# Turning layer 1's weights on VectorE and through DRAM instead of on TensorE, in the opening of a two-layer graph attention kernel

## The chip, the cores and the metric

The kernel runs on one core of a Trainium2 chip. A core has five engines that run their own instruction queues in order: TensorE (PE, matrix products into PSUM), VectorE (DVE), ScalarE (ACT), GpSimd (POOL) and SyncE (SP, which here issues every transfer). What counts is the device time of one execution in microseconds. Before the change it is 2786.34 us, the median of 3 runs (2786.06 to 2786.69).

## The reference

The input x is 128 graphs of 128 nodes with 512 features, in float32; adj is a 128x128 mask for each graph. Two attention layers follow each other.

```python
def _layernorm(x, eps=1e-5):
    return (x - mean(x)) / sqrt(var(x) + eps)

# layer 0: 4 heads of 64, INNER = 256
q, k, v = split_heads(x @ Wq), split_heads(x @ Wk), split_heads(x @ Wv)
attn = softmax(where(adj, q @ k.T / 8, -finfo.max))
x = _layernorm(x + (attn @ v) @ Wo + bo)

# layer 1: 8 heads of 64, INNER = 512, with a layer norm of its own in front
h = (x - mu) * rsqrt(var + 1e-5) * gamma + beta
q, k, v = split(h @ w_qkv.T, 3)
probs = softmax(where(adj | eye, q @ k.T / 8, -1e9))
x = _layernorm(x + (probs @ v) @ w_out.T + b_out)
```

Layer 0's weights come with the features along the rows, as TensorE wants them. Layer 1's w_qkv (1536x512) and w_out (512x512) are used transposed, so the kernel has to turn them once.

## The kernel before

The 128 graphs are 64 groups of G = 2. The order of all instructions is written out by hand (a manual schedule): every engine runs its own in the order in which the Python code emits them. `opening()` prepares weights and begins groups 0 and 1, `step(s)` runs for s from 2 to 63, and `closing` and `last` drain the pipeline. In step s, layer 0's q, k, v of group s are computed (`product_0`), with the softmax of group s - 1, the attention and output product of group s - 2 and its normalisation; layer 1's q and k of group s - 2 (`qk`), the softmax and v of group s - 3, and the attention and output product of group s - 4.

**Products with seven multiplications.** All projections use Strassen's scheme with Winograd's sums: a product of two-by-two blocks in seven block products instead of eight. `INTO` says into which PSUM bank each of the seven goes: 1, 6, 7 and 4 accumulate in bank a, 2 in bank c, 5 and 3 in bank f. The intermediate values are copied out between the accumulations: after product 1, ScalarE copies bank a to e1 (L387 in layer 0, L348 in layer 1, where the copies are called eqk or ev), and only then may product 6 accumulate into that bank. The scheme needs sums of input blocks, made by GpSimd for each group (`halves_sums`, L285: xs of the inputs, so of the attention's output), and sums of weight blocks, made once: four subtractions on VectorE (`combine`, L168 to L171) for layer 0's q, k, v weights, for each layer's output weights, and for layer 1's q, k and v weights. The first block is changed in place.

**Turning of weights.** `load_transposed` (L114) loads w_qkv and w_out in 16 row blocks of 128x512 into tiles that are free at the start (buffers of the groups' rows, tag r, and three others). Its `part(r)` turns one block: four TensorE transposes against the identity (L126) into one of four PSUM buffers, then one copy by ScalarE or VectorE (L130 to L134). `prepare(n)` takes n of these parts from a list. It stands six times in `opening` (12 blocks: q, k and v), and in step 2 takes the rest: gamma and beta (L143) and the four blocks of w_out.

**Turning of data, for groups after the first.** `turn` (L207) turns a group's rows in another way: VectorE transposes 32x32 blocks (L212) into a "turned" tile, of which there are two; SP writes it to DRAM (`put`, L197) and reads it back in four transfers that put the blocks in place (`fetch`, L203) into a "raw" tile, of which there is one; ScalarE brings it into order (L239 for layer 0, L251 for layer 1). Groups 0 to 2 of layer 0 and 0, 1 of layer 1 are turned by TensorE (`transposed`, L228; `finish_direct`, L263).

**Step 2 around layer 1's first product.** GpSimd's order is: so of group 0, the softmax's multiplication (L507), the roots for group 0's normalisation (L608 to L623), ratios, two memsets, xs of layer 1. ScalarE's norms (L634) wait for the roots, `finish_direct`'s transposes for the norms; ScalarE and VectorE then write xT, and `qk` begins with products 1, 2 and 6.

**Transfers.** The program gives transfers eight semaphores in turn, so the issue of each waits for the landing of the eighth before it.

## Time and profile before

| | |
|---|---|
| median of 3 runs | 2786.34 us |
| the profiled execution, its time | 2786.63 us |
| its span, first to last instruction | 2784.5 us |
| granted TensorE clock | 1.000 |
| busy PE / DVE / ACT / POOL | 2768.7 / 1795.3 / 1502.0 / 1747.4 us |
| DMA, mean over the span | 146 GB/s |
| opening, up to the first scores of step 2 | 0 to 38.46 us |
| step 2, up to step 3's last scores | 38.46 to 73.5 us |
| step 3 | 73.5 to 109.25 us |
| step 4, and each step after | 42.84 us |

The page has busy time by engine, the span in 40 slices, transfers, the chain of work that ended last (followed back from the last instruction), and groups of equal instructions. A timeline row has start, duration, engine, line, operation, output<-input, and in brackets the idle time before it with what ended it. A row of busy time by stage has the stretch, its length, then busy us of PE, PEld, DVE, ACT and POOL with the number of instructions, the granted clock, the busy share of the DMA engines and GB/s. In the first 110 us TensorE waits on others for about 4.7 us for the first rows and for 3.4 us more, in pieces of at most 1.0.

### The profile page before, as it was taken

To read this page: it belongs to the slowest core of one execution; us is meant where nothing else is said; L and a number is where in the kernel's file an instruction comes from. 1 tells how busy PE (TensorE), PEld (TensorE's weight loads), DVE (VectorE), ACT (ScalarE), POOL (GpSimd) and SP (SyncE) were. 2 spreads that over 40 slices of the span, in tenths; PEclk is the share of its full clock that TensorE was granted. 3 is DMA by queue.
4 is the path that set the end of the run, shared out by engine and by line. 5 is a ranking of instruction groups with operands and counts; after the bars stand their busy time and mean duration, and the time that the engine had idled before them with its cause. 6 is when DMAs were issued, how large, how long until landed. Compare 5 with 4: busy or idle time off the path is not lost.

```text
span 2784.5 us, 63222 instructions
## 1 busy us (share of the span) xinstructions
PE 2768.7 (99%) x23317; PEld 2609.6 (94%) x23317; DVE 1795.3 (64%) x3307; ACT 1502.0 (54%) x4811; POOL 1747.4 (63%) x2307
## 2 busy tenths in 40 slices
PE   8999999999999999999999999999999999999998
PEld 8999999999999999999999999999999999999997
DVE  5766666666666666666666666666666666666665
ACT  3555555645555556455555564555555645555554
POOL 4566566666665666666656666666566666666664
PEclk9999999999999999999999999999999999999999
DMA  5355454464454544645545445455454464554532
GB/s 169 109 144 165 129 165 148 127 176 140 143 165 128 166 148 127 179 137 143 164 127 168 147 129 175 139 145 165 127 167 146 129 177 135 147 163 128 160 107 69
DMA packets 281796, 405.24 MB, mean 146 GB/s; under 512 B 44680, under 2 KB 206480, under 8 KB 281488
## 3 DMA queue, kind: packets, MB, share of 16 engines
q1 hardware_dynamic: 281488, 401.20, 49.2%
q8 instruction: 185, 3.03, 0.5%
q14 instruction: 123, 1.01, 0.1%
HBM read 205.00 MB, written 196.08 MB: 144 GB/s over the span
## 4 chain that ended last, share of the span: by engine, by line
PE 96%; DVE 1%; issue 0%; POOL 0%; DMA 0%; ACT 0%; SPq 0%; POOLq 0%; ACTq 0%; DVEq 0%
PE qka L322 16%; PE a L378 12%; PE oa L416 12%; PE qkf L322 8%; PE va L322 8%; PE av L568 6%; PE f L378 6%; PE of L416 6%; PE qkc L322 4%; PE vf L322 4%; PE c L378 3%; PE oc L416 3%; PE sc L449 2%; PE sc L455 2%; PE vc L322 2%; PE sc_a L455 2%
## 5 line engine op out<-in xcount | busy, mean ns | idle before, releaser
L507 POOL TENSOR_TENSOR sm<-sm,rec 128x1024 f32<-128x1024 f32 x192 | 364.1, 1896 | 383.1 <-DVE rec L506 382.7
L498 ACT ACTIVATE sm<-sm,nmax 128x128 f32<-128x128 f32 x1536 | 595.4, 394 | 4.6 <-DVE nmax L489 3.7
L589 POOL TENSOR_TENSOR r<-r,bias 128x1024 f32<-128x1024 f32 x128 | 302.2, 2361 | 63.5 <-ACT r L588 63.5
L420 DVE TENSOR_TENSOR r<-oa,r 128x256 f32<-128x256 f32 x508 | 212.1, 418 | 200.3 <-PE oa L416 192.7
L285 POOL TENSOR_TENSOR xs<-xT 128x256 f32<-128x256 f32 x256 | 188.7, 737 | 218.3 <-ACT xT L239 165.1
L498 ACT ACTIVATION_READ_ACCUMULATOR sm<-sm,nmax 128x1 f32 x1536 | 295.9, 193 | 0.0
L348 ACT COPY eqk<-qka 128x512 f32<-128x512 f32 x128 | 74.9, 585 | 349.2 <-PE qka L322 349.2
L483 DVE COPY_PREDICATED sm<-m,sc 128x512 f32<-128x512 uint8 x256 | 172.8, 728 | 135.4 <-PE sc L449 134.9
L322 PE MATMUL qka<-xs,wsqk 128*128 128x128 f32 x2048 | 249.7, 275 | 0.1
L322 PE MATMUL qkf<-xs,w 128*128 128x128 f32 x2048 | 249.8, 275 | 0.0
L522 DVE STREAM_TRANSPOSE turnedp<-sm 128x1024 f32<-128x1024 f32 x189 | 233.9, 1238 | 15.2 <-DMA scrp<-turnedp 10.9
L322 PEld LDWEIGHTS qka<-xs,wsqk 128*128 128x128 f32 x2048 | 239.0, 192 | 0.3 <-POOL xs L285 0.3
L322 PEld LDWEIGHTS qkf<-xs,w 128*128 128x128 f32 x2048 | 239.0, 192 | 0.0
L353 DVE TENSOR_TENSOR qk<-qka,eqk 128x512 f32<-128x512 f32 x64 | 44.3, 691 | 290.4 <-PE qka L322 290.4
L489 DVE TENSOR_REDUCE nmax<-sm 128x8 f32<-128x1024 f32 x192 | 226.2, 1205 | 0.1
L416 PE MATMUL oa<-wso,so 128*128 128x256 f32 x760 | 206.0, 380 | 0.7 <-DVE r L420 0.7
L416 PE MATMUL of<-wo,so 128*128 128x256 f32 x760 | 205.5, 379 | 0.0
L608 POOL TENSOR_SCALAR ve<-mv 128x2 f32<-128x2 f32 x191 | 41.0, 214 | 261.5 <-DVE mv L601 255.4
L634 ACT ACTIVATE r<-r,shift,root 128x512 f32<-128x512 f32 x254 | 192.4, 807 | 8.7 <-POOL shift L623 4.7
L469 POOL MEMSET sm<- 128x1024 f32 x192 | 178.8, 951 | 0.0
L600 DVE BATCH_NORM_STATS2 st<-r 128x6 f32<-128x512 f32 x254 | 171.6, 676 | 4.4
L416 PEld LDWEIGHTS of<-wo,so 128*128 128x128 f32 x760 | 144.2, 190 | 19.9
(155 smaller groups left out, 6801.4 us busy)
## 6 DMA issues: line engine op xcount, KB each, us to landing
scrp<-turnedp SPq DMA_DIRECT2D x189, 512.0 KB, 3.2
pT<-scrp SPq DMA_DIRECT2D x756, 128.0 KB, 4.0
scr<-turned SPq DMA_DIRECT2D x121, 512.0 KB, 4.4
raw<-scr SPq DMA_DIRECT2D x484, 128.0 KB, 3.6
r<-in_x_dram SPq DMA_DIRECT2D x64, 512.0 KB, 3.9
out_dram<-r SPq DMA_DIRECT2D x63, 512.0 KB, 4.9
m<-in_adj_dram SPq DMA_DIRECT2D x64, 32.0 KB, 3.6
raw_r<-in_L_gnn_w_qkv_dram SPq DMA_DIRECT2D x8, 256.0 KB, 4.1
```

The costliest lines, as they stand in the source:

```text
L285: nc.gpsimd.tensor_tensor(o, a0, a1, op=op)
L322: nc.tensor.matmul(o, lhsT, rhs, start=first and n == 0, stop=n == len(todo) - 1, skip_group_check=True)
L378: nc.tensor.matmul(acc[:, t * P:(t + 1) * P], lhsT, rhs, start=first and n == 0, stop=n == len(todo) - 1, skip_group_check=True)
L416: nc.tensor.matmul(acc, left[:, c], right[:, c], start=first and c == 0, stop=c == hk - 1, skip_group_check=True)
L420: nc.vector.tensor_add(part, acc, part)
L469: nc.gpsimd.memset(sm, NEG1 if part else NEG0)
L489: nc.vector.tensor_reduce(NMAX[part], SM[part], AX.X, ALU.max, negate=True)
L498: nc.scalar.activation(sm[:, i, k, :], sm[:, i, k, :], AF.Exp, bias=nmax[:, i, k:k + 1], accum_out=total[:, i, k:k + 1])
L507: nc.gpsimd.tensor_tensor(SM[part], SM[part], rec[:, :, :, None].to_broadcast([P, 2, K1, N]), op=ALU.mult)
L522: nc.vector.transpose(t.rearrange("p q (h r) -> p q h r", r=32), SM.pop(part).rearrange("p i k (q r) -> p q (i k) r", r=32))
L589: nc.gpsimd.tensor_tensor(R[g], R[g], (bias0, bias1)[l][:, None, :].to_broadcast([P, G, E]), op=ALU.add)
L634: nc.scalar.activation(R[g][:, b], R[g][:, b], AF.Identity, bias=shift[:, b:b + 1], scale=root[:, b:b + 1])
```

## The change

The 64 transposes of layer 1's weights on TensorE are gone. The weights are loaded in eight pairs of row blocks (six of w_qkv, two of w_out). For each pair, `turn_rows` transposes it on VectorE and writes it to DRAM, `rows_arrive` reads it back into the one raw tile, and `rows_in_order` copies it into place on ScalarE. These three are placed by hand: pairs 0 and 1 (q) in `opening`, 2 and 3 (k) up to the middle of step 2, 4 and 5 (v) at the end of step 2, 6 and 7 (w_out) at the end of step 3. Group 0's q, k and v are computed by plain products (`plain_0`), which need no sums. The sums of layer 0's q and k weights and of layer 1's q and k weights are made on GpSimd, in whole tiles; v's and the output weights' stay on VectorE. Group 0's rows are loaded graph by graph, its mask after the weights, and the loads of wo, biases, gamma and beta stand later on SP.

```diff
@@ -61,16 +61,15 @@
 
     R, M = {}, {}
 
...
+    WROWS = [six.tile([P, 2, E], F32, tag="r", name=f"raw_{i}") for i in range(4)]
+    rows_ = one.tile([P, 4, E], F32, tag="qk1", name="raw_4")
+    WROWS += [rows_[:, :2], rows_[:, 2:]]
+    WROWS += [one.tile([P, 2, E], F32, tag=t, name=f"raw_{t}") for t in ("v1", "xT1")]
+
+    def load_rows(*pairs):
+        for i in pairs:
+            w, at = (w_qkv, i) if i < 6 else (w_out, i - 6)
+            nc.sync.dma_start(WROWS[i], w[at * 2 * P:(at + 1) * 2 * P].rearrange("(b p) e -> p b e", p=P))
 
     def load(g):
         if g >= NG:
@@ -80,7 +79,10 @@
         nc.sync.dma_start(R[g], x[g * G:(g + 1) * G].rearrange("b n e -> n b e"))
         nc.sync.dma_start(M[g], adj[g * G:(g + 1) * G].rearrange("b i j -> i b j"))
 
-    load(0)
+    R[0] = six.tile([P, G, E], F32, tag="r", name="r_0")
+    M[0] = six.tile([P, G, N], U8, tag="m", name="m_0")
+    for b in range(G):
+        nc.sync.dma_start(R[0][:, b], x[b])
 
 
     ident = const.tile([P, P], F32, name="ident")
@@ -97,46 +99,27 @@
     for h in range(2):
         for i, w in enumerate((wq, wk, wv)):
             nc.sync.dma_start(w0[:, :, h, i, :], w[:, h * HF:(h + 1) * HF].rearrange("(c p) f -> p c f", p=P))
+    nc.sync.dma_start(M[0], adj[:G].rearrange("b i j -> i b j"))
+    load_rows(0, 1, 2, 3)
     load(1)
     wo0 = const.tile([P, INNER[0] // P, E], F32, name="wo0")
-    nc.sync.dma_start(wo0, wo.rearrange("(c p) f -> p c f", p=P))
     bias0 = const.tile([P, E], F32, name="bias0")
-    nc.sync.dma_start(bias0, bo[None, :].to_broadcast([P, E]))
     bias1 = const.tile([P, E], F32, name="bias1")
-    nc.sync.dma_start(bias1, b_out[None, :].to_broadcast([P, E]))
 
     w1 = const.tile([P, KC, 3 * INNER[1]], F32, name="w1")
     wo1 = const.tile([P, INNER[1] // P, E], F32, name="wo1")
     gb_raw = const.tile([2 * KC, P], F32, name="gb_raw")
     gb = const.tile([P, 2 * KC], F32, name="gb")
 
-    setup = []
-    def load_transposed(dst, src, name, scaled=0):
...
-
-    nc.sync.dma_start(gb_raw[:KC], gamma.rearrange("(c p) -> c p", p=P))
-    nc.sync.dma_start(gb_raw[KC:], beta.rearrange("(c p) -> c p", p=P))
+    def wo0_and_bias():
+        nc.sync.dma_start(wo0, wo.rearrange("(c p) f -> p c f", p=P))
+        nc.sync.dma_start(bias0, bo[None, :].to_broadcast([P, E]))
+
+    def other_weights():
+        load_rows(4, 5, 6, 7)
+        nc.sync.dma_start(gb_raw[:KC], gamma.rearrange("(c p) -> c p", p=P))
+        nc.sync.dma_start(gb_raw[KC:], beta.rearrange("(c p) -> c p", p=P))
+        nc.sync.dma_start(bias1, b_out[None, :].to_broadcast([P, E]))
 
     def turn_gamma_beta():
         pt = mm_tile("gb_t")
@@ -154,46 +137,44 @@
     wsqk = const.tile([P, 3, KH, 2, I1 // 2], F32, name="wsqk")
     wsv = const.tile([P, 3, KH, I1 // 2], F32, name="wsv")
 
-    def weight_sums(w, ws, *blocks_):
...
-
-    def weight_sums_0():
-        combine(*(w0[:, c:c + KH, h].rearrange("p c t f -> p c (t f)") for c in (0, KH) for h in range(2)),
-                *(ws0[:, i].rearrange("p c t f -> p c (t f)") for i in range(3)))
+    def combine(eng, *sets):
+
+        for n in range(4):
+            for b11, b12, b21, b22, t2, t3, t4 in sets:
+                o, a, b = ((b12, b12, b11), (t2, b22, b12), (t3, t2, b11), (t4, b21, t2))[n]
+                eng.tensor_tensor(o, a, b, op=ALU.subtract)
+
+    def quarters(w, ws):
+
+        return (*(w[:, c:c + KH, h] for c in (0, KH) for h in range(2)), *(ws[:, i] for i in range(3)))
+
+    def weight_sums_qk(eng, t):
+        combine(eng, quarters(w1qk[:, :, t], wsqk[:, :, :, t]))
+
+    def weight_sums_v():
+        combine(nc.vector, quarters(w1v, wsv))
+
+    def weight_sums_0(eng, lo, hi):
+        combine(eng, tuple(t.rearrange("p c t f -> p c (t f)") for t in (
+            *(w0[:, c:c + KH, h, lo:hi] for c in (0, KH) for h in range(2)),
+            *(ws0[:, i, :, lo:hi] for i in range(3)))))
 
     WSO = tuple(const.tile([P, 3, i // P // 2, E // 2], F32, name=f"wso{l}") for l, i in enumerate(INNER))
 
     def weight_sums_out(l):
         hk = INNER[l] // P // 2
         w = (wo0, wo1)[l]
-        combine(*(w[:, c:c + hk, h * E // 2:(h + 1) * E // 2] for c in (0, hk) for h in range(2)),
-                *(WSO[l][:, i] for i in range(3)))
-
-    load_transposed(w1, w_qkv, "w_qkv", scaled=INNER[1])
-    setup.append(turn_gamma_beta)
-    load_transposed(wo1, w_out, "w_out")
+        combine(nc.vector, (*(w[:, c:c + hk, h * E // 2:(h + 1) * E // 2] for c in (0, hk) for h in range(2)),
+                            *(WSO[l][:, i] for i in range(3))))
 
     WO = (wo0, wo1)
     RATIO, XT, QK, V, QKV = {}, {}, {}, {}, {}
 
 
 
-    def put(t, name):
-
-        scr = dram.tile(list(t.shape), F32, tag=name.split("_")[0], name=name)
+    def put(t, name, bufs=2):
+
+        scr = dram.tile(list(t.shape), F32, tag=name.split("_")[0], bufs=bufs, name=name)
         nc.sync.dma_start(scr, t)
         return scr
 
@@ -218,6 +199,25 @@
             return
         RAW[l] = one.tile([P, 4, G, KC, 32], F32, tag="raw", name=f"raw{l}_{g}")
         fetch(RAW[l].rearrange("p a b c i -> p a (b c i)"), SCR[l])
+
+
+    def turn_rows(*pairs):
+        for i in pairs:
+            t = one.tile([P, 4, G * KC * 32], F32, tag="turned", bufs=2, name=f"turnedw_{i}")
+            for b in range(2):
+                nc.vector.transpose(t.rearrange("p a (b c i) -> p a b c i", b=2, c=KC)[:, :, b],
+                                    WROWS[i][:, b].rearrange("p (c a i) -> p a c i", a=4, i=32))
+            SCR["w", i] = put(t, f"scrw_{i}", 8)
+
+    def rows_arrive(i):
+        RAW["w"] = one.tile([P, 4, 2, KC, 32], F32, tag="raw", name=f"raww_{i}")
+        fetch(RAW["w"].rearrange("p a b c i -> p a (b c i)"), SCR.pop(("w", i)))
+
+    def rows_in_order(i):
+        w, at = (w1, i) if i < 6 else (wo1, i - 6)
+        for b in range(2):
+            o = w[:, :, (2 * at + b) * P:(2 * at + b + 1) * P].rearrange("p c (a j) -> p a c j", a=4)
+            nc.scalar.activation(o, RAW["w"][:, :, b], AF.Copy, scale=SCALE if i < 2 else 1.0)
 
     def transposed(g):
 
@@ -228,7 +228,8 @@
                 nc.tensor.transpose(pt[:, c * N:(c + 1) * N], R[g][:, b, c * P:(c + 1) * P], ident)
             (nc.scalar.copy, nc.vector.tensor_copy)[b](xT[:, :, b * N:(b + 1) * N],
                                                        pt.rearrange("p (c n) -> p c n", c=KC))
-        sums(0, g)
+        if g > 0:
+            sums(0, g)
 
     def in_order(g):
 
@@ -390,6 +391,24 @@
             else:
                 b, h, e = {2: (0, 0, 1), 3: (0, 1, 6), 7: (1, 1, 5)}[i]
                 nc.vector.tensor_add(whole(b, h), src, EV[0, e])
+
+    def plain_0(*what):
+
+        xT = XT[0, 0]
+        for kind, i in what:
+            acc = mm_tile(f"plain_{kind}{i}")[:, :2 * P]
+            for c in range(KC):
+                lhsT, rhs = ((xT[:, c, i * N:(i + 1) * N], w0[:, c, :, 2]) if kind == 2 else
+                             (w0[:, c, i, kind], xT[:, c]))
+                nc.tensor.matmul(acc, lhsT, rhs, start=c == 0, stop=c == KC - 1)
+            acc = acc.rearrange("p (x n) -> p x n", x=2)
+            if kind == 0:
+
+                nc.scalar.activation(QKV[0][:, :, i, 0], acc, AF.Copy, scale=SCALE)
+            elif kind == 1:
+                nc.vector.tensor_copy(QKV[0][:, :, i, 1], acc)
+            else:
+                nc.scalar.copy(QKV[0][:, i, :, 2], acc)
 
 
     def out_product(l, g, *which):
@@ -684,47 +703,48 @@
         for i in which:
             product("qk", g, i)
 
-    def prepare(n):
-        for _ in range(min(n, len(setup))):
-            setup.pop(0)()
-
     def opening():
 
+        QKV[0] = two.tile([P, G, 2, 3, P], F32, tag="qkv0", name="qkv0_0")
+        cleared(1, 0)
         transposed(0)
-        cleared(1, 0)
-
+        turn_rows(0, 1)
+        wo0_and_bias()
+        plain_0((0, 0), (1, 0), (0, 1))
+        turn_rows(2)
+        rows_arrive(0)
+        plain_0((1, 1), (2, 0))
+        turn_rows(3)
+        load(2)
+        other_weights()
         for h in range(2):
             nc.scalar.activation(w0[:, :, h, 0, :], w0[:, :, h, 0, :], AF.Copy, scale=SCALE)
-        product_0(0, 1)
-        weight_sums_0()
-        product_0(0, 2, 5, 6, 3)
-        prepare(2)
-        load(2)
-        product_0(0, 7)
-        prepare(2)
-        product_0(0, 4)
-        transposed(1)
+        weight_sums_0(nc.gpsimd, 0, 2)
 
         made = scores(1)
+        plain_0((2, 1))
         masked(made, 1, 0)
         maxima(1, 0)
+        transposed(1)
+        weight_sums_0(nc.vector, 2, 3)
+        rows_in_order(0)
+        rows_arrive(1)
+        exps(1, 0, 0)
         product_0(1, 1, 2)
-        exps(1, 0, 0, 1)
-        prepare(2)
+        exps(1, 0, 1)
         normalised(1, 0)
         product_0(1, 6, 5)
-        prepare(2)
         weight_sums_out(0)
+        rows_in_order(1)
+        rows_arrive(2)
         addend(0, 0)
-        product_0(1, 7)
-        prepare(2)
+        product_0(1, 7, 3)
         blocks_direct(1, 0)
         cleared(2, 0)
-        weight_sums(w1qk, wsqk, 0)
-        product_0(1, 3)
-        prepare(2)
+        weight_sums_qk(nc.gpsimd, 0)
         product_0(1, 4)
         transposed(2)
+        turn_rows(4, 5)
 
     def step(s):
 
@@ -740,6 +760,9 @@
         if s > 3:
             maxima(s, 1)
         out_sums(0, s - 2)
+        if s == 2:
+            rows_in_order(2)
+            rows_arrive(3)
         exps(s, 0, 0)
         product_0(s, 1)
         exps(s, 0, 1)
@@ -747,6 +770,8 @@
         if s == 3:
             maxima(s, 1)
         maxima(s, 2)
+        if s == 2:
+            turn_rows(6, 7)
         product_0(s, 2)
         normalised(s, 0)
         out_product(0, s - 2, 6, 3)
@@ -754,6 +779,10 @@
         stats(0, s - 2, 0)
         product_0(s, 6)
         exps(s, 1, 1)
+        if s == 2:
+            rows_in_order(3)
+            rows_arrive(4)
+            weight_sums_qk(nc.gpsimd, 1)
         out_product(0, s - 2, 7)
         product_0(s, 5)
         out_product(0, s - 2, 4)
@@ -767,7 +796,10 @@
         flush()
         product_0(s, 4)
         if direct:
-            prepare(len(setup))
+            if s == 2:
+                turn_gamma_beta()
+            else:
+                rows_arrive(6)
         else:
             turn(1, s - 2)
         out_sums(1, s - 4)
@@ -790,7 +822,11 @@
         else:
             finish(s - 2, 0)
         if s == 2:
-            weight_sums(w1qk, wsqk, 1)
+            rows_in_order(4)
+            rows_arrive(5)
+        if s == 3:
+            rows_in_order(6)
+            rows_arrive(7)
         out_product(1, s - 4, 6, 5)
         if not direct:
             finish(s - 2, 1)
@@ -799,6 +835,10 @@
         probs_arrive(s, 1)
         stats(1, s - 4, 0)
         stats(1, s - 4, 1)
+        if s == 2:
+            rows_in_order(5)
+        if s == 3:
+            rows_in_order(7)
         arrive(0, s + 1)
         probs_arrive(s, 2)
         cleared(s + 1, 2)
@@ -810,7 +850,7 @@
         addend(1, s - 3)
         qk(s - 2, 7, 3, 4)
         if s == 2:
-            weight_sums(w1v, wsv, 0, 1)
+            weight_sums_v()
         if s == 3:
             weight_sums_out(1)
```

More of the change, by code (lines that the diff above doesn't have):

```diff
@@ L62 @@
     R, M = {}, {}
-    spare = []
-    def spare_rows(pool, tag, n):
-        rows_n = pool.tile([P, n, E], F32, tag=tag, name=f"raw_{tag}_{len(spare)}")
-        spare.extend(rows_n[:, i] for i in range(n))
-    for i in range(4):
-        spare_rows(six, "r", 2)
-    for tag, n in (("qk1", 4), ("v1", 2), ("xT1", 2)):
-        spare_rows(one, tag, n)
+    WROWS = [six.tile([P, 2, E], F32, tag="r", name=f"raw_{i}") for i in range(4)]
[6 more added lines that the diff above has]
+            nc.sync.dma_start(WROWS[i], w[at * 2 * P:(at + 1) * 2 * P].rearrange("(b p) e -> p b e", p=P))
     def load(g):
@@ L111 @@
     gb = const.tile([P, 2 * KC], F32, name="gb")
-    setup = []
-    def load_transposed(dst, src, name, scaled=0):
-        rows, cols = src.shape
-        raws = []
-        for r in range(rows // P):
-            raw = spare.pop(0)
-            nc.sync.dma_start(raw, src[r * P:(r + 1) * P, :])
-            raws.append(raw)
-        def part(r):
-            raw = raws[r]
-            pt = mm_tile(f"{name}t_{r}")
-            for c in range(cols // P):
-                nc.tensor.transpose(pt[:, c * P:(c + 1) * P], raw[:, c * P:(c + 1) * P], ident)
-            to = dst[:, :, r * P:(r + 1) * P]
-            pt = pt.rearrange("p (c f) -> p c f", f=P)
-            if r * P < scaled:
-                nc.scalar.activation(to, pt, AF.Copy, scale=SCALE)
-            elif r % 2:
-                nc.scalar.copy(to, pt)
-            else:
-                nc.vector.tensor_copy(to, pt)
-        setup.extend(lambda r=r: part(r) for r in range(rows // P))
-    nc.sync.dma_start(gb_raw[:KC], gamma.rearrange("(c p) -> c p", p=P))
-    nc.sync.dma_start(gb_raw[KC:], beta.rearrange("(c p) -> c p", p=P))
+    def wo0_and_bias():
[6 more added lines that the diff above has]
+        nc.sync.dma_start(bias1, b_out[None, :].to_broadcast([P, E]))
     def turn_gamma_beta():
@@ L155 @@
     wsv = const.tile([P, 3, KH, I1 // 2], F32, name="wsv")
-    def weight_sums(w, ws, *blocks_):
-        for c in blocks_:
-            if w is w1qk:
-                b11, b12 = w[:, c, :, 0], w[:, c, :, 1]
-                b21, b22 = w[:, KH + c, :, 0], w[:, KH + c, :, 1]
-            else:
-                b11, b12 = w[:, c, 0], w[:, c, 1]
-                b21, b22 = w[:, KH + c, 0], w[:, KH + c, 1]
-            combine(b11, b12, b21, b22, ws[:, 0, c], ws[:, 1, c], ws[:, 2, c])
-    def combine(b11, b12, b21, b22, t2, t3, t4):
-        nc.vector.tensor_sub(b12, b12, b11)
-        nc.vector.tensor_sub(t2, b22, b12)
-        nc.vector.tensor_sub(t3, t2, b11)
-        nc.vector.tensor_sub(t4, b21, t2)
-    def weight_sums_0():
-        combine(*(w0[:, c:c + KH, h].rearrange("p c t f -> p c (t f)") for c in (0, KH) for h in range(2)),
-                *(ws0[:, i].rearrange("p c t f -> p c (t f)") for i in range(3)))
+    def combine(eng, *sets):
[13 more added lines that the diff above has]
+            *(ws0[:, i, :, lo:hi] for i in range(3)))))
     WSO = tuple(const.tile([P, 3, i // P // 2, E // 2], F32, name=f"wso{l}") for l, i in enumerate(INNER))
```

## The prediction

> **What bounds the kernel now.** I read the page first (busy time, then the chain that ended last), then busy time by stage, then the first 110 us instruction by instruction.

> ```profile
> PE 2768.7 (99%) x23317; PEld 2609.6 (94%) x23317; DVE 1795.3 (64%) x3307; ACT 1502.0 (54%) x4811; POOL 1747.4 (63%) x2307
> ...
> PE 96%; DVE 1%; issue 0%; POOL 0%; DMA 0%; ACT 0%; SPq 0%; POOLq 0%; ACTq 0%; DVEq 0%
> ```

> TensorE holds 96% of the chain. So only two things move the end: TensorE work, and stretches in which TensorE waits. The stages (columns: stretch, its length, then busy us of PE, PEld, DVE, ACT, POOL) are the opening, steps 2 and 3, and step 4:

> ```profile
> 4.70:38.46 33.76, 32.47 (x265) 31.14 (x265) 19.28 (x27) 14.29 (x38) 11.90 (x12) 1.00 0.74 247
> 38.46:73.50 35.04, 33.72 (x310) 32.13 (x311) 25.95 (x49) 13.27 (x36) 19.02 (x26) 1.00 0.25 77
> 73.50:109.25 35.75, 34.69 (x276) 32.01 (x272) 24.27 (x44) 18.70 (x68) 22.76 (x28) 1.00 0.45 125
> 109.25:152.09 42.84, 42.84 (x365) 40.47 (x364) 29.17 (x54) 23.49 (x75) 27.30 (x36) 1.00 0.50 143
> ```

> From step 4 on PE has no idle time (42.84 of 42.84 us), and the change doesn't touch those steps. Whatever shift stands at 109.25 us, where step 4 begins, stands at the end. The ledger is therefore only of the first 109 us. The place that decides most is the start of layer 1's q,k products in step 2 (timeline):

> ```profile
> 57.38 1.51 ACT L268 ACTIVATE xT<-ht,gb 128x128 f32<-128x128 f32 x4
> ...
> 57.90 2.18 PE L322 MATMUL qka<-xT,w 128*128 128x128 f32 x16 [0.16 <-ACT xT L268]
> ...
> 59.91 1.95 PE L322 MATMUL qkc<-xT,w 128*128 128x128 f32 x16
> ...
> 60.17 0.59 ACT L348 COPY eqk<-qka 128x512 f32<-128x512 f32 x1 [1.28 <-PE qka L322]
> ...
> 62.00 2.05 PE L322 MATMUL qka<-xs,wsqk 128*128 128x128 f32 x16
> ```

> Product 1 fills bank qka, product 2 another bank, and product 6 accumulates into qka again. It may not start before ScalarE has copied product 1 out (eqk, L348). Here that copy is done by 60.8, so it costs nothing.

> [...]a 128x256 subtraction, 0.42 us elsewhere, takes 2.47 beside a GpSimd addition of 2.54:

> ```profile
> 30.91 2.54 POOL L589 TENSOR_TENSOR r<-r,bias 128x1024 f32<-128x1024 f32 x1
> ...
> 31.27 2.47 DVE L169 TENSOR_TENSOR wso<-wo 128x256 f32<-128x256 f32 x1
> ```

> [...]Here the smallest read-back needs 2.5 us from issue to landing (the line of L203):

> ```profile
> L203 SPq DMA_DIRECT2D raw<-scr x484: 302/429/1666, 63.4 to 2661.4; - x162
> ...
> DMA to landing us min/median/max: 2.5/3.9/5.7
> ```

> [...]the first a product's 8 matmuls at 7.02 take 2.08 us, the same 8 take 1.16 at 22.71.

> **The change, part by part** (us on before's clock).

> *TensorE work.* 64 transposes go: 16 blocks of four at 0.49 (8 records in 1.04 pitch 0.98) = 7.8; 5.9 of it in the opening, 1.9 in step 2. Group 0's seven products (7 x 1.34 = 9.4) become six plain ones of four 128x256 matmuls (L416 has two such records in 0.43, so 24 x 0.43 = 10.3). Net 6.9 us less work; before also loses 1.0 and 0.7 us to VectorE's weight copies (waits at 39.97 and 35.66). That is the most there is to gain: about 8.6.

> *Opening.* The turning is a chain: load, VectorE transpose (2 x 0.67 by L212), write to DRAM, read back in four transfers, ScalarE reorder (two copies, 1.14 by L239). Two "turned" buffers mean that pair 2 is transposed only when pair 0's write has landed. On SP's queue that write stands behind four 0.52 MB loads, r_1 and a mask. In before Wv landed at 10.9 and loads then ran at 371 to 390 GB/s: 3.2 MB more = 8.4, so 19.3. VectorE turns pair 2 until 20.6, and behind it waits the k copy that the first scores need: scores at 21.0 against 21.62. The products of group 0 themselves are hidden in this. ScalarE now does pair 0's reorder ahead of the exps: read-back lands about 26, so reorder until 27.3, half the exps (1.55) and the copy of product 1 until 29.4, where before it was 24.9. Product 6 of group 1 starts at 29.4 against 26.36; 8.5 us of PE work follow, with 1.2 of waits on VectorE's wo subtractions[...]. The step-2 attention starts at about 40.2 against 41.06: **-0.9**. Of the 5.9 + the waits saved, nearly all is spent waiting.

> *GpSimd, first sums.* Pair 1's read-back stands behind 4.7 MB of 0.52 MB transfers plus 0.3 MB after pair 0's write. At 0.38 MB/us, one read-back at its slower rate (221 GB/s in 104:109, +0.9), its last quarter issues at 33.4 and lands at 36.5; reorder until 37.7. GpSimd's four subtractions of 128x512: rows give 0.46 at 128 columns, 0.73 at 256, 2.36 at 1024, so 1.27 each, 5.3 with gaps: until 43.0. Behind them wait xs (3.2) and so: first so at 46.7. TensorE's third out product wanted it at 44.39. TensorE, there at 43.5, waits 3.2 us, and product 6 of group 2 is at 49.35 against 47.02, the shift now +2.3: **+3.2**. The 1.27 is from rows of other widths; it can't be under the 0.73 of half the width nor over the 1.90 of twice it (L507), so four of them are between 3.0 and 7.8, and the wait between 1 and 6. [...]VectorE's turning of pairs 6 and 7 (2.55) stands in front of the residual adds, on which the seventh out product waits: another **+0.5**, shift +2.8.

> *GpSimd, second sums.* After the normalise (ends about 52.8) four more subtractions, until 58.1, ahead of the roots. Their chain (52.23 to 53.79) ends at 59.7, ScalarE's norms follow, and finish_direct's copies end at 63.2 against 58.89, shift +4.3: **+1.5**, with the 1.9 of missing transposes already in it. Behind the roots on GpSimd stand ratios, two memsets (1.84) and xs; xs still comes before product 6 in its new place.

> *Two round trips.* In step 2 ScalarE has, between those copies and eqk: reorder of pair 4 (1.15); only then the one raw buffer is free and the four read-backs of pair 5 issue (1.4 to the last, +2.9 landing, 4.4 with the hand-over); reorder (1.15); then eqk (0.5). That is 7.2 after the copies' end. Product 2 ends 2.97 after it (61.86 - 58.89). So TensorE stands still for 4.2 us, **+4.1** over before's 0.14. Step 3 does the same with pairs 6 and 7: product 6 was at 100.15, copies' end 97.34 + 7.2 = 104.55: **+4.4**.

> The landing can be 2.5 to 4 us instead of 2.9, so each stall is 3.8 to 5.5.

> *The rest.* v sums in four pieces of 0.69 for eight of 0.43: **-0.4**, VectorE being on the chain there. At nothing I put four edits. The split first load: the turning chain hides it. Mask 0 behind the weights: about 12, wanted at 22. wo, its bias and r_2, now held on SP behind writes that wait for VectorE: about 22 and 29, wanted at 30.6 and 38; each us later than that would cost one. In step 3 SP holds the probabilities' read-backs behind pair 7's, which waits for ScalarE: some 2 us later, wanted 10 us on. GpSimd's first sums (group 0's weights, 16.4 to 21.7) are wanted at 29.4. Half-rate clock[...]: from 0 to about 2 for each of three or four; I take **+1.6** in all.

> Sum: -0.9 +3.2 +0.5 +1.5 +4.1 +4.4 -0.4 +1.6 = +14.0. The span 2784.5 becomes 2798.5. The profiled execution took 2786.63, 2.1 around the span; the runs' median is 2786.34, so 1.84: 2800.3.

> **Rivals.** (a) *Feeds on time*: the transfers of pair 1 land some 6 us earlier and GpSimd's queue stays hidden; then only the round trips count: -0.9 -1.9 +4.1 +4.4 -0.4 = +5.3, 2791.6. For: SP's queue is idle from 25 to 55 in before. Against: the DMA share there is 1.04 until 28 without the added 3 MB. (b) *Faster*: every read-back has landed when ScalarE asks for it, so TensorE's own work sets the pace: the 8.6 us above, 2777.7. The mechanism is the landing time alone, its place the two eqk copies. Pairs 5 and 7 would have to land within about 0.1 us of the issue for no stall; the sign turns where the waits that come in (8.5 in the two stalls alone) fall under the 8.6 of work and waits removed, and less than 3 us of them may be left for 0.2%. Against: 2.5 is the minimum of the 1240 read-backs of L203. (c) *Nothing*: gain and stalls cancel, 2786. (d) *Worse*: written and read-back traffic holds the 221 GB/s for the whole opening, pair 1 is 3 us later, and each long stall pays the full half-rate stretch: +22, 2808. That the turning leaves TensorE is certain from the program's order.

> **How the numbers follow.** Forecast 0.62, (a) 0.13, (b) 0.05, (c) 0.05, (d) 0.15. A measurement tells 0.2% (5.6 us) from no change. Half of (a) and all of (c) are within: same 0.11; faster 0.05; slower 0.84. Range 2790 to 2809, reaching over (a) and (d); the forecast's own is 2795 to 2805.

> **What would show it.** Right: TensorE idle before product 6 of step 2 and of step 3, released by ScalarE's eqk copy, 4 to 6 us each; scores(1) near 21; so late in step 2; step 4's start at about 122 us, and 42.84 us per step after it. Wrong: no idle before those products; pair 1's reorder done by 32; or a step 4 that starts before 109.

## The result, and the profile after

The changed kernel takes **2807.36 us** (median of 4 runs, 2805.98 to 2809.73), beside 2786.52 for the kernel before (2786.06 to 2787.40): a ratio of **1.0075, 95% interval 1.0062 to 1.0088**. The forecast was 2800.3, range 2790 to 2809: sign and range held, the size was 7 us short. The profiled execution took 2805.98, its span 2804.1 against 2784.5 before: +19.6.

From the page of the changed kernel: busy time, the granted clock in 40 slices (the row called PEclk), the chain by engine.

```profile
PE 2772.3 (99%) x23217; PEld 2610.4 (93%) x23217; DVE 1794.3 (64%) x3304; ACT 1504.6 (54%) x4817; POOL 1758.3 (63%) x2315
...
PEclk8999999999999999999999999999999999999999
...
PE 95%; DVE 0%; ACT 0%; issue 0%; POOL 0%; POOLq 0%; ACTq 0%; DVEq 0%
```

TensorE has 100 instructions fewer and yet 3.6 us more of busy time. The counts can't say why; the first digit of the clock can. It is an 8: part of the first 70 us ran at less than the full clock. The chain says as little as it did before, since all the damage is in less than 5% of the span.

Busy time by stage shows where (stretch, length, then PE, PEld, DVE, ACT, POOL with their instructions, granted clock, DMA share, GB/s): everything up to step 4's first scores, and step 4.

```profile
0.00:129.53 129.53, 104.68 (x741) 95.82 (x742) 68.15 (x116) 49.77 (x148) 65.49 (x80) 0.91 0.62 193
129.53:172.40 42.87, 42.87 (x365) 40.50 (x364) 29.41 (x54) 23.49 (x75) 27.32 (x36) 1.00 0.47 135
```

Step 4 takes 42.87 us with TensorE never idle, as before (42.84). So the loss lies ahead of it: step 4 starts at 129.53 where it started at 109.18, **+20.35** (behind it single steps of one kernel or the other take 0.3 to 0.4 us more, so that +19.6 of it stand in the span). In those 129.53 us TensorE is idle for 24.85. What it waits for there (waiting for: us in all, times, longest):

```profile
PE qka L323 <- ACT eqk L349: 7.6, 2, 4.5
PE sc L468 <- DVE qkv L409: 3.7, 1, 3.7
PE of L435 <- POOL so L286: 3.7, 1, 3.7
PE xt L228 <- DMA r<-in_x_dram: 3.6, 1, 3.6
PE ht L264 <- ACT r L653: 3.1, 1, 3.1
```

The fourth is the wait for the first rows, which the kernel before has too. The other four are waits that the prediction names: product 6 behind the round trip (twice), the first scores behind the turning, the out product behind GpSimd's first sums, `finish_direct` behind its second sums. The start of layer 1's products in step 2, the place shown for the kernel before, now reads so in the timeline:

```profile
66.60 1.51 ACT L269 ACTIVATE xT<-ht,gb 128x128 f32<-128x128 f32 x4
...
67.21 3.68 PE L323 MATMUL qka<-xT,w 128*128 128x128 f32 x16
...
67.99 1.15 ACT L220 ACTIVATE w<-raww 128x512 f32<-128x512 f32 x2
70.69 2.33 PE L323 MATMUL qkc<-xT,w 128*128 128x128 f32 x16
74.31 1.15 ACT L220 ACTIVATE w<-raww 128x512 f32<-128x512 f32 x2 [5.17 <-DMA raww<-scrw]
75.37 0.57 ACT L349 COPY eqk<-qka 128x512 f32<-128x512 f32 x1
76.08 2.02 PE L323 MATMUL qka<-xs,wsqk 128*128 128x128 f32 x16 [3.06 <-ACT eqk L349]
```

Follow ScalarE down the rows: the reorder of pair 4, then 5.17 us of nothing until pair 5's read-back has landed, the reorder of pair 5, and only then eqk, whose input was complete when product 1 ended at 70.9. And product 1 takes 3.68 us, where it took 2.18.

### The profile page after: what moved, and what is told of

Read it like the earlier page. It is cut to its first block, busy times and chain, and to the rows that moved or that the text cites. A ratio compares the mean times of both kernels' runs of the same rounds, so it can differ in the third digit from the quotient of the medians.

```text
span 2804.1 us, 63080 instructions
## 1 busy us (share of the span) xinstructions
PE 2772.3 (99%) x23217; PEld 2610.4 (93%) x23217; DVE 1794.3 (64%) x3304; ACT 1504.6 (54%) x4817; POOL 1758.3 (63%) x2315
## 4 chain that ended last, share of the span: by engine, by line
PE 95%; DVE 0%; ACT 0%; issue 0%; POOL 0%; POOLq 0%; ACTq 0%; DVEq 0%
PE qka L323 16%; PE a L379 12%; PE oa L435 12%; PE qkf L323 8%; PE va L323 8%; PE av L587 6%; PE f L379 6%; PE of L435 6%; PE qkc L323 4%; PE vf L323 4%; PE oc L435 3%; PE c L379 3%; PE sc L468 2%; PE sc L474 2%; PE vc L323 2%; PE sc_a L474 2%
```

## The experiments

Each was timed beside the kernel before on the same chip; ratios are to that. Unless said otherwise, the edit is to the changed kernel (2807.36; 1.0075 [1.0062, 1.0088]), and the diff is against it.

### Is the eqk copy late because of the last pair?

The reorder of the last pair in steps 2 and 3 is put behind the copies of products 1 and 6, and with it the read-back of the next group's rows (`arrive`), which goes into the same raw tile.

```diff
-        if s == 2:
-            rows_in_order(5)
-        if s == 3:
-            rows_in_order(7)
-        arrive(0, s + 1)
+        if not direct:
+            arrive(0, s + 1)
...
         qk(s - 2, 1, 2, 6)
+        if direct:
+            rows_in_order(5 if s == 2 else 7)
+            arrive(0, s + 1)
         flush()
```

> Pairs 5 and 7 are put in order behind products 1, 2 and 6 of layer 1's q,k, so ScalarE's eqk copy no longer stands behind a read-back; the transfers, buffers and all amounts of work stay. Round-trip theory: TensorE's waits of 3.06 us (step 2) and 4.54 us (step 3) before product 6 go, and with the second one the half-rate stretch behind it (clock 0.5 from 115.5 to 122.8 in the changed kernel, some 2.1 us of matmul time): about -9.7 us against the changed kernel, near 2797.5. Rival (another wait is just behind: xs on GpSimd or the next raw read-back, which now issues later): less than -4, near 2804.

Measured **2793.79** (11 runs, 2792.01 to 2795.50), 1.0024 [1.0015, 1.0034]: 13.6 us below the changed kernel. Its timeline at the same place:

```profile
69.54 0.58 ACT L349 COPY eqk<-qka 128x512 f32<-128x512 f32 x1 [1.74 <-PE qka L323]
71.07 1.95 PE L323 MATMUL qka<-xs,wsqk 128*128 128x128 f32 x16
...
73.94 1.15 ACT L220 ACTIVATE w<-raww 128x512 f32<-128x512 f32 x2 [0.23 <-DMA raww<-scrw]
```

ScalarE copies eqk as soon as product 1 has ended, product 6 follows product 2 without a gap, and pair 5, reordered 4.4 us later, still comes in time. The two waits were the largest part of the loss, as forecast. They cost 3.9 us more than the expected 9.7. The clock may be where that comes from, though no run parts it from the waits: in the changed kernel the granted clock is down to a half for stretches that add up to 11.9 us of lost clock in the first 130 us (some of it while TensorE is idle), here to 3.4; the mean clocks of the other executions agree (0.995 or 0.996 in the four of the changed kernel, 0.997 or 0.998 in these eleven).

### Is it the landing, or ScalarE's own copying?

Here the reorders stay in front of eqk, but the last pair has a raw tile of its own and is read back together with the pair before it.

```diff
-        RAW["w"] = one.tile([P, 4, 2, KC, 32], F32, tag="raw", name=f"raww_{i}")
+        RAW["w", i] = one.tile([P, 4, 2, KC, 32], F32, tag=("raw", "pT2")[i % 2], name=f"raww_{i}")
...
             rows_arrive(4)
+            rows_arrive(5)
...
                 rows_arrive(6)
+                rows_arrive(7)
...
             rows_in_order(4)
-            rows_arrive(5)
         if s == 3:
             rows_in_order(6)
-            rows_arrive(7)
```

> Odd pairs get a second raw buffer (the still unused one of pT2), and pairs 5 and 7 are read back one reorder earlier; ScalarE's order stays as in the changed kernel, with both reorders ahead of the eqk copy. Round-trip theory: it is the wait for the landing that costs, not the 1.15 us of a reorder on ScalarE: 1.15 + 1.15 + 0.5 after the end of finish_direct's copies is 2.8 us, under the 3.0 that products 1 and 2 take from there; so the same -9.7 us, near 2797.5, within 1.5 of the run that moves the reorder. Rival (ScalarE's work itself is the cost): the two reorders stay in front of the copy and at most half of it comes back, near 2803.

Measured **2794.82** (6 runs, 2793.14 to 2795.34), 1.0028 [1.0016, 1.0040], not to be told from the kernel above. Product 6 of step 2 is at 71.62. So the wait was for a landing that could not be asked for sooner, there being one raw tile. ScalarE's two reorders of 1.15 us fit beside products 1 and 2: in step 3, where the clock is whole, product 6 starts at 109.15, 3.80 us behind product 1, as in the kernel before (100.15 and 96.35).

### The second sums back on VectorE

```diff
             rows_arrive(4)
-            weight_sums_qk(nc.gpsimd, 1)
...
         if s == 2:
+            weight_sums_qk(nc.vector, 1)
             rows_in_order(4)
             rows_arrive(5)
```

> The second half of layer 1's q,k weight sums is made by VectorE behind finish_direct, where the kernel before has it, instead of by GpSimd ahead of the roots. GpSimd-queue theory: roots start at 59.7 instead of 63.0, TensorE's wait before ht (3.07 us at 65.4) goes and its half-rate stretch moves; the copies' end and so product 6 come 3.3 us earlier: -3.3 us, or only -1.3 if the then longer wait before product 6 makes the clock fall there instead. Near 2804 to 2806. Rival (the roots are not what ht waits for[...]): no change, 2807.

Measured **2807.74** (4 runs, 2807.36 to 2809.08), 1.0077 [1.0062, 1.0092]: nothing gained; the expectation of the theory failed. The step that it speaks of did happen. `finish_direct` transposes at 60.81 in place of 65.45, with no wait. Then, in the timeline:

```profile
62.97 1.16 ACT L220 ACTIVATE w<-raww 128x512 f32<-128x512 f32 x2
63.85 2.00 SPq L184 DMA_DIRECT2D pT<-scrp  x4
...
65.97 0.36 SPq L178 DMA_DIRECT2D scr<-turned  x1
66.45 2.29 SPq L184 DMA_DIRECT2D raww<-scrw  x4
72.51 1.15 ACT L220 ACTIVATE w<-raww 128x512 f32<-128x512 f32 x2 [8.39 <-DMA raww<-scrw]
...
74.28 3.75 PE L323 MATMUL qka<-xs,wsqk 128*128 128x128 f32 x16 [8.22 <-ACT eqk L349]
```

The raw tile is free at 64.1, but SP has the probabilities' read-back and a write of layer 0's rows ahead in its queue; pair 5's four transfers issue from 66.45, and product 6 waits 8.22 us in place of 3.06. The raw tile is free 5.0 us sooner than in the changed kernel, but the four transfers begin only 2.7 sooner and have landed 1.8 sooner. So product 6 starts 1.8 us sooner, and as it and product 5 then run at half rate (3.75 and 2.60), that goes too: step 3's scores are at 85.72 for 85.18. The wait for the roots had covered a wait for SP's queue and for the landing. So the forecast's +1.5 for the second sums was right for the row where it was put and worth nothing at the end, as long as the round trip stands behind it.

### GpSimd's first sums behind `so`

```diff
-        weight_sums_qk(nc.gpsimd, 0)
         product_0(1, 4)
...
         out_sums(0, s - 2)
         if s == 2:
+            weight_sums_qk(nc.gpsimd, 0)
             rows_in_order(2)
```

> The first half of those sums is issued on GpSimd behind xs and so of step 2 instead of ahead of them. GpSimd-queue theory: TensorE's wait of 3.69 us for so (at 50.1) goes with the half-rate stretch behind it (1.7 us); but both sums then stand together before the roots, GpSimd ending them about 59.7 instead of 62.9, so ht comes 3.2 us earlier, not 5.4: -3.2 us, near 2804. Rival (the first sums are hidden, the wait comes from xs): no change.

Measured **2803.96** (4 runs, 2801.10 to 2805.57), 1.0062 [1.0047, 1.0077]: 3.4 lower by the medians, 3.2 expected, though the intervals overlap. The trace bears it out: the out product's wait of 3.69 is gone (the product is at 45.44), and the profiled span is 4.8 shorter.

### The k copy ahead of the turning

```diff
         plain_0((0, 0), (1, 0), (0, 1))
+        plain_0((1, 1), (2, 0))
         turn_rows(2)
         rows_arrive(0)
-        plain_0((1, 1), (2, 0))
         turn_rows(3)
```

> Pair 2 is transposed behind the k copy of group 0 instead of ahead of it, so the first scores don't wait for pair 0's write to land. Turned-buffer theory: the wait of 3.70 us before scores(1) (at 21.15) and its half-rate stretch (20.3 to 27.1) go, product 6 of group 1 comes 1 to 2 us earlier; but step 2 begins when pair 1's read-back is in order (41.4), which stays: 0 to -1 us in the end, near 2807. Rival (the opening's waits add up to the end): -5 us, near 2802.

Measured **2806.42** (4 runs, 2804.14 to 2811.44), 1.0072 [1.0057, 1.0087], no difference that can be told. The first scores run at 16.53 without a wait, 4.6 us sooner, but TensorE then waits 2.7 us for an `e` copy, because ScalarE stands in front of pair 0's reorder; step 2's scores come at 39.99 against 40.79. The opening is bound by the read-back of pair 0, as the forecast had it: an early start is spent waiting later.

### What the half clock costs

Needless matmuls, whose results nothing reads, are put where TensorE would stand still: ahead of the first scores, of out product 5 and of `finish_direct` in step 2, and between products 2 and 6 of steps 2 and 3. Nothing else changes.

```diff
+    def busy(n, tag, name):
+        t = ps_st.tile([P, 512], F32, tag=tag, name=f"busy_{name}")
+        for i in range(n):
+            nc.tensor.matmul(t[:, :384], ident, w0[:, 0, 0].rearrange('p t f -> p (t f)')[:, :384], start=True, stop=True)
...
+        busy(4, "f", "o")
...
+            busy(4, "f", "of")
...
+                busy(3, "f", "ht")
...
+            busy(6 if s == 2 else 4, "f0", f"qk{s}")
...
```

> TensorE gets needless matmuls (128x384, results unread) into its five long waits (opening 4, before so's product 4, before ht 3, before product 6 6 and 4), short enough to end before the wait does; all else as in the changed kernel. Clock theory: the granted clock stays at 1.0, the waits end when they did, and what follows them runs at full rate: -1.7 us behind so, -1 behind ht, -2.1 in step 3, nothing in the opening: about -4 to -5 us, near 2803, though TensorE does more work. Rival (the half rate is hidden in the next wait, or the needless work delays what follows): 0 or slower, 2807 or more.

Measured **2803.45** (4 runs, 2801.95 to 2804.65), 1.0059 [1.0044, 1.0074]: 3.9 lower by the medians (the intervals overlap), with more work on TensorE. In the profiled execution the granted clock shows no stretch below 1.00 in the first 130 us; the three others have a mean of 0.998, so some half clock was left in them. The same four-microsecond stretches, first in the changed kernel and then in this one (columns as above; the granted clock is the third number from the end):

```profile
20.00:24.00 4.00, 2.85 (x15) 2.45 (x16) 3.40 (x7) 0.00 (x0) 3.67 (x3) 0.53 0.83 280
24.00:28.00 4.00, 3.73 (x14) 2.85 (x13) 1.62 (x3) 0.99 (x3) 0.00 (x0) 0.61 0.92 282
```

```profile
20.00:24.00 4.00, 2.38 (x21) 2.01 (x20) 3.96 (x7) 0.85 (x2) 2.90 (x3) 1.00 0.68 244
24.00:28.00 4.00, 3.72 (x31) 3.38 (x30) 3.71 (x6) 0.96 (x2) 3.74 (x4) 1.00 0.98 287
```

From 24 to 28 TensorE is as busy in both, but starts 14 matmuls in one and 31 in the other (not all of one shape). Cut at marks, the gain has two places: product 6 of group 2 comes 1.9 us sooner (52.59 for 54.50), and step 3 needs 9.1 us from its product 6 to step 4 instead of 11.1. Product 6 of step 3, in the changed kernel and in this one:

```profile
118.39 3.76 PE L323 MATMUL qka<-xs,wsqk 128*128 128x128 f32 x16 [4.54 <-ACT eqk L349]
```

```profile
116.87 2.02 PE L323 MATMUL qka<-xs,wsqk 128*128 128x128 f32 x16 [1.77 <-ACT eqk L349]
```

The two other stretches of half clock give nothing back. In the opening, pair 0's read-back lands only at 28.7 here, so that product 6 of group 1 starts at 31.93, no sooner than in the changed kernel (31.06); in step 2 product 6 still waits 1.83 us for eqk, and the half clock only fills time in which TensorE would have waited.

### Plain products alone

The kernel before, with group 0's products made plain (with the copies as in the change) and layer 0's weight sums behind them, on VectorE as they were.

```diff
+        plain_0((0, 0), (1, 0), (0, 1), (1, 1), (2, 0))
+        prepare(2)
+        load(2)
+        plain_0((2, 1))
         for h in range(2):
             nc.scalar.activation(w0[:, :, h, 0, :], w0[:, :, h, 0, :], AF.Copy, scale=SCALE)
-        product_0(0, 1)
         weight_sums_0()
-        product_0(0, 2, 5, 6, 3)
...
```

> The kernel before with one part of the change alone: group 0 by plain products, layer 0's weight sums after them on VectorE; weights still turned on TensorE. It does 1.3 us more on TensorE in place of the waits in products 1 to 4 for sums and xs. Theory: the opening isn't bound there by more than 1 us: between -1.5 and +1.5 us against before, 2785 to 2788. Rival (the plain products are a gain of their own, the loss of the whole change is then larger elsewhere): -3 or more.

Measured **2789.62** (12 runs, 2788.52 to 2790.21), 1.0009 [1.0000, 1.0018], 3.1 above the kernel before on its chip (2786.50) by the medians, outside what was expected; the interval just reaches 1. VectorE's rows show one part of it:

```profile
23.47 0.96 DVE L168 TENSOR_TENSOR w<-w 128x768 f32<-128x768 f32 x1 [5.36 <-DMA raw_v<-in_L_gnn_w_out_dram]
...
27.20 0.68 DVE L229 COPY xT<-xt 128x512 f32<-128x512 f32 x1
```

Plain products read the unscaled, unsummed weights, so scaling and sums, in place, move behind them. The DMA that the row names serves other data; what ends just then is ScalarE's scaling of the weights (22.29 to 23.44). The four sums, 3.8 us, were made at 10.91 before, beside products; now they stand in front of VectorE's copy of group 1's xT, which was at 21.79. From the first scores to step 2's attention product it is now 22.0 us for 19.4. Another part lies ahead of that: the first scores come at 23.98 for 21.62, late before the sums stand in anyone's way, and the plain products are 0.9 us more work by the prediction's sum. So both the sums' new place and the products cost something; no run parts the two. In the full change GpSimd has the q and k part of them.

### All moves together

The separate raw tiles, both moves of GpSimd's sums, the k copy; and pair 1 is read back ahead of the loads of pairs 4 to 7, each reorder of pairs 0 and 1 behind the softmax and the products that need ScalarE. Of its diff, parts of the opening:

```diff
         plain_0((0, 0), (1, 0), (0, 1))
+        plain_0((1, 1), (2, 0))
         turn_rows(2)
         rows_arrive(0)
-        plain_0((1, 1), (2, 0))
+        rows_arrive(1)
         turn_rows(3)
...
-        rows_in_order(0)
-        rows_arrive(1)
...
         normalised(1, 0)
+        rows_in_order(0)
+        rows_arrive(2)
...
         transposed(2)
+        rows_in_order(1)
+        rows_arrive(3)
         turn_rows(4, 5)
...
```

> The changed kernel with every found wait taken out together: k copy ahead of pair 2; second raw buffer and read-backs issued early, pair 1's ahead of the loads of pairs 4 to 7; reorders of pairs 0 and 1 behind the copies that TensorE waits for; first sums behind so; second sums on VectorE behind finish_direct. If these waits are the whole loss, what is left is TensorE's smaller work: step 4 begins 3 to 7 us before the kernel before's 109.2, 2779 to 2784. Rival (turning through DRAM is too slow for the place whatever the order: the k weights are not in order by product 1 of step 2): step 2 waits for pair 3, 2787 to 2795.

Measured **2785.25** (12 runs, 2782.67 to 2787.72), 0.9996 [0.9987, 1.0004]: the same as before, between the two expectations. The waits for eqk, `so` and the roots are gone, and step 2's scores come at 36.26, 2.2 us ahead of the kernel before; step 4 starts only 0.5 ahead (108.70 against 109.18). The loss is in step 2:

```profile
45.16 1.30 DVE L208 STREAM_TRANSPOSE turnedw<-raw_v 128x512 f32<-128x512 f32 x2 [1.95 <-DMA scrw<-turnedw]
...
48.64 1.19 PE L435 MATMUL oa<-wso,so 128*128 128x256 f32 x2 [2.20 <-DVE r L439]
49.62 1.91 PE L379 MATMUL f<-xs,w 128*128 128x128 f32 x8
```

VectorE stands in front of the turning of pairs 6 and 7 until the writes of pairs 4 and 5 have left the two turned tiles, and behind it stand the residual adds. TensorE waits 2.20 and runs the next products at half rate (1.91 for 1.05).

### The turning of pairs 6 and 7 later

To the kernel with all moves:

```diff
-        if s == 2:
-            turn_rows(6, 7)
         product_0(s, 2)
...
         out_product(0, s - 2, 7)
+        if s == 2:
+            turn_rows(6, 7)
         product_0(s, 5)
```

> Like the kernel with all moves together (2785.25), but VectorE turns pairs 6 and 7 behind the residual adds of the seventh out product instead of ahead of those of the third. My account of that kernel: TensorE's 2.20 us wait at 48.64 for a residual add, which stands behind the turning (1.95 us for a buffer that is being written, then 2.5 us of transposes), and the half-rate stretch behind it (1.7 us of clock) are what keep its step 2 from being ahead of the kernel before. Then both go, the norms come some 2 to 3 us earlier, gamma and beta are turned near 54 instead of 56.67, and the kernel takes about 2782 us (2780.5 to 2783.5), clearly under the kernel before. The rival: the wait only hides the next one (ScalarE's e copies behind a reorder, or the turning now ahead of the last residual add), so that gamma and beta stay within 0.7 us of 56.67 and the time stays at 2784.5 to 2786.

Measured **2785.08** (21 runs, 2783.98 to 2787.08) beside 2787.70 for the kernel before (25 runs): **0.9991 [0.9984, 0.9997]**. It beats both kernels, the one before by 2.6 us, less than a tenth of a per cent; from the kernel with all moves (0.9996 [0.9987, 1.0004]) its interval doesn't part it. The expected 2782 was not reached. The wait did shrink:

```profile
47.82 0.67 PE L435 MATMUL oa<-wso,so 128*128 128x256 f32 x2 [0.57 <-DVE r L439]
48.32 1.05 PE L379 MATMUL f<-xs,w 128*128 128x128 f32 x8
```

But gamma and beta are turned at 55.25 in place of 56.67, 1.4 us sooner instead of 2 to 3, since waits for an e copy (1.1), for VectorE's sums (0.8) and for the norms (0.3) take their part; and a half-rate stretch, gone from step 2, stands at 23.5 to 27 in this execution, where step 2's scores come at 36.80 against 36.26. Step 4 starts 1.0 us sooner. Neither expectation was quite right: the time lies where the rival had it, though on a chip on which the kernel before is 1.2 us slower, and gamma and beta lie between the two. The cause was named; about half of its price was already owed elsewhere.

## Why the prediction was right, and where its sizes failed

The sign and the places of the waits were right, and the sizes of most. The measured 2807.36 lies outside the forecast's own 2795 to 2805, and inside the range because that was drawn wide enough for rival (d). The forecast's sum was +14.0; step 4 came +20.35 later. Cut at the instructions that both the prediction and the trace name (start times; the shift is against the kernel before):

| up to | before | forecast | measured | added, forecast | added, measured |
|---|---|---|---|---|---|
| step 2's attention product | 41.06 | 40.2 | 42.93 | -0.9 | +1.9 |
| product 6 of group 2 | 47.02 | 49.35 | 54.50 | +3.2 | +5.6 |
| end of `finish_direct`'s copies | 58.89 | 63.2 | 68.11 | +2.0 | +1.7 |
| product 6, step 2 | 62.00 | 70.4 | 76.08 | +4.1 | +4.9 |
| product 6, step 3 | 100.15 | 112.55 | 118.39 | +4.0 | +4.2 |
| step 4 | 109.18 | 123.2 | 129.53 | +1.6 | +2.1 |

The forecast's column is its terms (+2.0 is +0.5 and +1.5; +4.0 is +4.4 and -0.4; its half-rate +1.6 is put in the last row for want of a place; its text said "about 122" for step 4, where its own sum gives 123.2).

- **The two round trips, +4.1 and +4.4: right**, by cause too: removed in two ways, they give 12.5 and 13.6 us back, half clock included. In step 2 eqk ends 7.8 us after the copies, forecast 7.2; the four read-backs took 2.5 to issue for 1.4, the landing 2.6 for 2.9.
- **The opening, -0.9: failed by 2.8.** The mark that it names, product 6 of group 1, is at 31.06 for 29.4. Pair 0's reorder begins at 27.86 for about 26, right behind ScalarE's copy of group 1's xT, which is late because the last plain product (3.78 for 1.89) and the transposes (1.43 for 1.04) ran at half rate. Yet in the run without half clock the read-back itself landed no sooner than 28.7. Either of the two holds product 6 near 31, and the runs don't part them. From there to the attention product it is 11.9 us where 10.8 were reckoned (8.5 of work and 1.2 of waits; the 1.1 of step 2's scores is in the prediction's sum, not in its words).
- **"Half-rate clock ... I take +1.6": mis-sized, 3.9.** Two stretches lie on the path: 51 to 54.4, in front of product 6 of group 2, and the one behind product 6 of step 3 (3.76 and 2.30 for 1.95 each). The run without half clock gives 1.9 and 2.0 back just there, and 3.9 in all. The term was the author's estimate, with no recorded stretch in the first 110 us of the trace before to size it by. A wait's length doesn't decide: the stretch from 64.6 on set in during a wait of 3.07, one of 3.06 had none behind it, and the last section shows what tells the cases apart. And the doubled duration at 7.02, 2.08 us for 1.16, is not shown to be half clock: that trace's record of the granted clock begins only at 10.95.
- **GpSimd's first sums, +3.2: right at the end, by two errors that cover each other.** Each subtraction took 1.27 to 1.28, as worked out. But pair 1's reorder began at 40.23, forecast 36.5: the last quarter of the read-back issued at 35.16 (33.4), and took 5 us to land (3.1). So `so` was 3.4 late against the forecast. TensorE came 2.8 late too, and the wait between them was 3.69 for 3.2; the rest of the +5.6 is the half clock behind it. Rows by microsecond, with the rate last, show the slow landing:

```profile
34.00:35.00 1.00, 1.00 (x11) 1.00 (x11) 1.00 (x1) 0.48 (x1) 1.00 (x2) 1.00 1.04 392
35.00:36.00 1.00, 1.00 (x11) 1.00 (x11) 0.96 (x2) 0.00 (x0) 1.00 (x1) 1.00 1.12 237
36.00:37.00 1.00, 1.00 (x11) 1.00 (x11) 1.00 (x1) 0.00 (x0) 1.00 (x1) 1.00 1.09 200
```

  While loads run, 392 GB/s; as the read-backs come up, 237 and 200 at the same busy share. Between 20 and 28, with writes and read-backs among the loads, the rate is 281, where the forecast reckoned with 380: 0.8 MB that had to come later. No run took the mixture alone apart, so that it is the mixture, and not the order on the queues, is read from these rows and not shown.
- **The second sums, +1.5, and the turning of pairs 6 and 7, +0.5: right as sizes** (+1.7 for both together), but the run with those sums moved shows that they cover the round trip behind them, and so are no cost that can be saved alone.
- **"Nearly all is spent waiting": right**, as the run with the k copy moved shows; the first scores, forecast at 21.0, were at 21.15.
- **The rivals.** Rival (d), "pair 1 is 3 us later, and each long stall pays the full half-rate stretch", 2808, is nearest to what came, and should have had more than 0.15, though only two of the four stretches cost their full time and its "whole opening at 221 GB/s" was too strong. (b) needed landings within 0.1 us of the issue: after its last issue the pair of step 2 took 2.6. (a) failed on pair 1's landing and on the half clock. "The products of group 0 themselves are hidden" was not tested in the full change; alone, going plain costs 3.1 us.

## What to carry to other kernels

Work moved off a full TensorE on to a chain of transpose, write, read-back and reorder pays only if the next link can be asked for before the last is consumed: here one raw tile put a landing of some 5 us in front of a copy that TensorE wanted, twice. Price a stall with the clock behind it: by the two profiled executions, two of the four stretches here cost 1.9 and 2.0 us beyond the waits, the two that lay under another wait nothing. And before giving one wait a price, ask what it covers, since two of the repairs here gained nothing until the next wait was repaired as well.
